# A graph layer's edge groups with a window of 97 nodes instead of 96

## The chip, the cores and the metric

The kernel runs on one core of a Trainium2 chip. The metric is the device time of one execution in microseconds (us), as the median of several runs. The core has five engines that run their own instruction streams and meet by semaphores: TensorE (PE, with its weight loads as PEld), VectorE (DVE), ScalarE (ACT), GpSimd (POOL) and SyncE (SP), and 16 DMA engines that SP, ACT and POOL feed through queues.

## The reference

One message-passing layer on a graph of 6250 nodes and 100000 edges, with features of width 128 and four attributes an edge, all in float32. Edges are sorted by their destination. Cut to what is computed:

```python
msg_in = concatenate([x[src], x[dst], edge_attr], axis=1)      # 100000 x 260
h = silu(msg_in @ mW1 + mb1)
messages = h @ mW2 + mb2
aggregated = segment_sum(messages, dst, num_segments=6250)
u = silu(concatenate([x, aggregated], axis=1) @ uW1 + ub1)
g = layer_norm(x + u @ uW2 + ub2, ln_g, ln_b)
out = layernorm(x + g)
```

## The kernel before

The first product is taken apart: `x @ mW1` is computed per node, once for the part of the source (table A) and once for the part of the destination (table B, with the bias). Both tables are written to DRAM, `tab_a` and `tab_b` (L394, L395), in seven parts of up to eight blocks of 128 nodes. After that an edge needs row A of its source, row B of its destination, and the product of its four attributes with four rows of `mW1`.

The edges are cut into 98 groups of 1024, each eight tiles of 128 edges. Because the edges are sorted, the destinations of a group lie in a window of `W` consecutive nodes that begins at the first edge's destination (`bases[g]`, a register on SP and DVE). `W` is 96. The window serves twice:

- On the way in, rows B are not gathered per edge. The window's `W` rows are loaded into `mv[g % 5][:W]` (L590), below them stand the four rows of `mW1` for the attributes. The matching matrix `stbuf[g % 5]` has `W` rows of 0 and 1 that say which edge goes to which node (`node_matrix`, L595, on DVE), and the four attribute rows of the group's edges under them (L591). One product per tile on PE (L622) gives the destination's part and the attributes' part together, over 100 rows.
- On the way out, `edge_matrix` (L608, DVE) makes the same matrix with edges on the partitions, and PE sums the messages' hidden rows `h` by node (L651), 96 columns a tile. The result is added into `acc` at the window's place (L664), the counts into `deg` (L669).

If a group's destinations go beyond the window, or a node batch would close too early, `bad_i` is set (L239 to L265), and a general path after the last group does the whole work again; with these inputs it is not entered.

What feeds this: `destinations` (L319) loads, for four groups at once, one byte an edge from `near_d`, 4096 bytes in a row, and repeats that row on all `W` partitions of the tile `near` (L324, two buffers). It is issued by SP ahead of the first of its groups' loads. `load(g)` (L584) issues the rows of B and the attributes four groups ahead. All of these go over SP's DMA queue, in SP's order, beside the node batches' loads (L499) and stores (L563) and the attributes' turning (L310, L317). A load into a buffer waits until its last reader is done.

Rows of A are gathered by POOL, one indirect DMA a tile (L281), so eight a group and 782 in all, 128 rows of 512 bytes each. `fetch(g + 2)` is issued in turn `g` of the loop over groups, and two dependencies are put on it by hand: its first gather waits for the first product of group `g + 2`, its fifth for the first summing product of group `g`. The gathers of POOL use eight semaphores in turn.

In turn `g` of the loop (L679 to L723) the order on the engines is written out by hand: the loads of group `g + 4`; the sum of gathered rows and product, `s = ga + pre` (L639, DVE), and its SiLU (L640, ACT); the products of group `g + 2` (L622, PE), whose PSUM buffer is free once `s` is computed; `node_matrix(g + 3)` and `edge_matrix(g + 1)` (DVE); the addition of group `g - 2`; the summing products of group `g` (L651, PE); then `fetch(g + 2)`. Batches of finished nodes (`node_batch`, L470) run in steps between. The first five groups are handled apart: they gather rows of `x` itself, and PE turns and multiplies them (L365, L373, L625), so that they need not wait for table A. From group 5 (`RAW`) on table A is read.

The change touches the constant `W` (L76) and, through it, the sizes of `p_next`, `w_row`, `zeros`, `acc`, `deg`, `deg_q`, `near`, `mv`, `stbuf`, `oh` and `pt`.

Of the kernel before, what the change touches and what calls it, by code (L numbers as in the profile page):

```python
# [24 lines left out]
def kernel(  # L25
# [47 lines left out]
    GE = G * P  # L73
    NG = -(-E // GE)
    assert NG <= P
    W = 96  # L76
    NW = NP + W
    K1 = W + ED
    RB = 14
# [95 lines left out]
    make_identity(nc, ident)  # L175
    w_row_i = consts.tile([P, W], I32, name="w_row_i")
    nc.gpsimd.iota(w_row_i, pattern=[[1, W]], base=0, channel_multiplier=0)

    w_row = fixed.tile([P, W], F32, name="w_row")
    nc.vector.tensor_copy(w_row, w_row_i)  # L180
# [3 lines left out]
    nc.vector.tensor_copy(p_col, p_col_i)  # L184
    p_next = consts.tile([W, 1], F32, name="p_next")
    nc.vector.tensor_scalar(p_next, p_col[:W], 1.0, None, op0=OP.add)
# [733 lines left out]
```

## Time and profile before

| | |
|---|---|
| median of three runs | 1205.35 us (1204.87 to 1210.69) |
| profiled execution | 1207.88 us |
| its span, first to last instruction | 1206.1 us |
| mean granted TensorE clock | 0.654 |
| busy: PE / DVE / ACT / POOL | 762.4 / 488.4 / 245.3 / 742.2 us |
| gathers L281, mean | 948 ns |
| loads of B (L590): number, size each | 98, 48 KB |
| loads of destinations (L324): number, size each | 24 of 384 KB and one of 192 KB |
| `node_matrix` L595, mean | 1269 ns |
| `edge_matrix` L608, mean | 949 ns |
| product L622 / summing product L651, mean of one pass | 394 / 350 ns |

A float32 product counts as two passes in the profile, so L622 and L651 have 1564 each for 782 tiles. Line numbers (L281) are those of the kernel's source. "Idle before" is the time that an engine stood still ahead of an instruction, with what ended it; "issue" means that nothing visible did, "remote" that the releasing event could not be traced to an instruction. DMA packets are recorded with queue, size, start and duration, but without the number of the DMA engine: q0 is POOL's queue, q1 SP's, q10 ACT's.

### The profile page before, as it was taken

The page shows a single profiled execution, that of the slowest core. Times are in us where ns is not written, and L with a number is a line of the kernel's source. Part 1 is how long each engine was busy: PE and PEld are TensorE (multiplying, and loading weights), DVE is VectorE, ACT ScalarE, POOL GpSimd, SP SyncE. Part 2 cuts the span into 40 slices and gives each one's busy share as a digit, 9 for nine tenths or more (in the row PEclk, how much of TensorE's full clock was granted, in tenths as well). Part 3 has the DMA queues.
Part 4 walks back from the last instruction along what each step waited for, and adds up shares of the span by engine and source line. Part 5 has one row for each costly group of instructions (what it writes and reads, how often), then busy time and mean ns, then how long its engine had stood idle before and what let it go on. Part 6 is the DMA issues. An engine that isn't in the chain of part 4 may idle for free.

```text
span 1206.1 us, 11356 instructions
## 1 busy us (share of the span) xinstructions
PE 762.4 (63%) x3655; PEld 682.4 (57%) x3655; DVE 488.4 (40%) x1023; ACT 245.3 (20%) x306; POOL 742.2 (62%) x790
## 2 busy tenths in 40 slices
PE   4656588665665766575566675666676657566564
PEld 4555577565555655465466465555566547455553
DVE  4450356353253344335335244334334326235253
ACT  1202024013022222212112122102202202112233
POOL 6446356666666666666666666666666666666660
PEclk8877777865756666666756656666655665765665
DMA  8553123212222322222222223222212312222210
GB/s 204 163 150 88 29 61 91 67 51 78 74 64 62 80 66 64 78 66 61 74 72 60 72 54 82 75 62 64 80 50 78 82 51 72 75 53 63 57 49 28
DMA packets 70221, 88.95 MB, mean 74 GB/s; under 512 B 20720, under 2 KB 51839, under 8 KB 70155
## 3 DMA queue, kind: packets, MB, share of 16 engines
q0 software_dynamic: 25024, 51.30, 16.4%
q1 hardware_dynamic: 40552, 34.96, 10.1%
q10 hardware_dynamic: 4578, 1.89, 0.7%
q8 instruction: 31, 0.51, 0.2%
q14 instruction: 36, 0.29, 0.1%
HBM read 76.71 MB, written 11.38 MB: 73 GB/s over the span
## 4 chain that ended last, share of the span: by engine, by line
PE 33%; issue 33%; POOL 15%; DVE 7%; another core or an unknown queue 7%; DMA 2%; ACT 1%; SPq 0%; ACTq 0%; DVEq 0%; POOLq 0%
POOL ga L281 15%; PE pre L622 14%; PE pt L651 12%; PE y L529 2%; DVE oh L608 1%; DMA ga<-tab_a,src_i 1%; DVE st L595 1%; PE wide L388 1%; PE y L520 1%; DVE st L487 1%; PE y L513 1%; DVE s L639 1%; PE y L514 1%; DVE deg L669 1%
## 5 line engine op out<-in xcount | busy, mean ns | idle before, releaser
L281 POOL DMA_INDIRECT ga<-tab_a,src_i x742 | 703.1, 948 | 406.2 <-issue 201.5
L622 PE MATMUL pre<-mv,st 100*128 100x128 f32 x1564 | 342.5, 394 | 243.0 <-issue 202.6
L622 PEld LDWEIGHTS pre<-mv,st 100*128 100x128 f32 x1564 | 312.6, 298 | 264.8 <-issue 227.4
L651 PE MATMUL pt<-oh,h 128*128 128x96 f32 x1564 | 294.6, 350 | 128.4 <-issue 119.3
L651 PEld LDWEIGHTS pt<-oh,h 128*128 128x128 f32 x1564 | 280.0, 266 | 146.1 <-issue 140.7
L639 DVE TENSOR_TENSOR s<-ga,pre 128x1024 f32<-128x1024 f32 x92 | 112.2, 1219 | 500.1 <-DMA ga<-tab_a,src_i 425.0
L640 ACT ACTIVATE h<-s 128x1024 f32<-128x1024 f32 x92 | 97.0, 1056 | 688.8 <-issue 424.4
L595 DVE TENSOR_SCALAR_CACHE_REDUCE st<-near,p_next 96x1024 f32<-96x1024 uint8 x98 | 124.2, 1269 | 3.0 <-DMA ea_d<-pad 1.5
L608 DVE TENSOR_TENSOR oh<-w_row,rel 128x768 f32<-128x768 f32 x98 | 93.0, 949 | 0.6 <-PE pt L651 0.6
L281 POOL DMA_INDIRECT ga<-in_x_dram,src_i x32 | 30.3, 946 | 24.4 <-PE wide L365 12.4
L531 DVE TENSOR_TENSOR y<-y,xs 128x512 f32<-128x512 f32 (+2 forms) x13 | 8.4, 647 | 86.6 <-issue 71.0
L640 ACT ACT_TABLE_LOAD x25 | 32.1, 1283 | 22.5 <-remote 17.6
L388 PE MATMUL wide<-w,xT 128*128 128x256 f32 x98 | 29.0, 462 | 11.4 <-ACT xT L344 7.3
L493 ACT ACT_TABLE_LOAD x26 | 33.4, 1283 | 4.4 <-DVE st L487 3.9
L388 PEld LDWEIGHTS wide<-w,xT 128*128 128x128 f32 x98 | 23.0, 241 | 16.2 <-ACT xT L344 7.5
L529 PEld LDWEIGHTS y<-u,uT 128*128 128x128 f32 x94 | 22.6, 324 | 11.9 <-issue 11.8
L518 ACT ACTIVATE uT<-y,ub_col 128x512 f32<-128x512 f32 (+2 forms) x13 | 8.4, 646 | 89.3 <-remote 62.2
L664 DVE TENSOR_TENSOR acc<-acc,pt 128x96 f32 x98 | 23.7, 242 | 5.7 <-remote 3.8
L529 PE MATMUL y<-u,uT 128*128 128x128 f32 x94 | 25.7, 429 | 0.0
L669 DVE TENSOR_TENSOR deg<-deg,pt 1x96 f32 x98 | 24.4, 249 | 1.0
L488 DVE BATCH_NORM_AGGREGATE mv<-st 128x2 f32<-128x6 f32 x98 | 17.8, 182 | 11.6 <-DVE st L487 5.5
L625 PE MATMUL pre<-w,ga 128*128 128x128 f32 x80 | 20.6, 344 | 3.0 <-issue 2.9
(122 smaller groups left out, 381.3 us busy)
## 6 DMA issues: line engine op xcount, KB each, us to landing
ga<-tab_a,src_i POOLq DMA_INDIRECT x742
near<-near_d SPq DMA_DIRECT2D x24, 384.0 KB
mv<-tab_b SPq DMA_DIRECT2D x98, 48.0 KB
tab_a<-t SPq DMA_DIRECT2D x6, 512.0 KB
tab_b<-x_sb SPq DMA_DIRECT2D x6, 512.0 KB
xs<-in_x_dram SPq DMA_DIRECT2D x11, 256.0 KB
out_dram<-z SPq DMA_DIRECT2D x11, 256.0 KB
st<-ea_d SPq DMA_DIRECT2D x98, 16.0 KB
```

Source lines behind the costliest of these rows:

```text
L281: ins = nc.gpsimd.indirect_dma_start(out=rows[g][:, i, :], out_offset=None, in_=x if g < RAW else tab_a[:, :], in_offset=bass.IndirectOffs ...
L388: ins = nc.tensor.matmul(pm[:, j], xT[:, cols], w1, start=True, stop=True)
L493: nc.scalar.activation(r[:, :n], mv[:, :n, 1], AF.Sqrt, bias=eps)
L529: nc.tensor.matmul(y[:, i, :], by_p[:, :, i], u2, start=False, stop=i == n - 1)
L595: nc.vector.tensor_scalar(stbuf[g % NST][:W], near.pop(g), p_next, 0.0, op0=OP.is_equal, op1=OP.add, accum_out=deg_q[g // DQ % 2][:, g % D ...
L608: nc.vector.tensor_tensor(oh, w_row[:, None, :].to_broadcast([P, G, W]), rel[:, g, :, None].to_broadcast([P, G, W]), op=OP.is_equal,)
L622: ins = nc.tensor.matmul(pre[:, i, :], st[:, i, :], mv[g % NM], start=True, stop=g >= RAW)
L639: nc.vector.tensor_add(s[:, :n], ga[:, :n], ps[:, :n])
L640: nc.scalar.activation(h[:, :n], s[:, :n], AF.Silu)
L651: ins = nc.tensor.matmul(pt[:, :W], h[:, i, :], oh[:, i, :], start=i == 0, stop=i == tiles_of(g) - 1)
L664: nc.vector.tensor_add(at, at, pt[:, :W])
L669: nc.vector.tensor_add(at, at, pt[row, W:])
```

## The change

One constant grows by one: a group's window holds 97 nodes instead of 96. Every tile, DMA and instruction that has `W` rows or columns gets 97; their number, their order on each engine and the waits between them stay as they are. Loads of B go from 96 rows of 512 bytes to 97, loads of destinations from 96 rows of 4096 bytes to 97. The product L622 runs over 101 rows, the summing product L651 has 97 columns, `edge_matrix` 776 elements a partition.

```diff
     NG = -(-E // GE)
     assert NG <= P
-    W = 96
+    W = 97
     NW = NP + W
     K1 = W + ED
     RB = 14
```

## The prediction

> **What bounds the kernel now.** I read the page first (busy shares, DMA queues, chain), then the waits, then POOL's timeline in the long middle stage, then the packet records behind the DMA view. Busy shares and DMA of the page:
>
> ```profile
> span 1206.1 us, 11356 instructions
> PE 762.4 (63%) x3655; PEld 682.4 (57%) x3655; DVE 488.4 (40%) x1023; ACT 245.3 (20%) x306; POOL 742.2 (62%) x790
> ...
> q0 software_dynamic: 25024, 51.30, 16.4%
> q1 hardware_dynamic: 40552, 34.96, 10.1%
> ```
>
> No engine is full, and the 16 DMA engines are a quarter full (26.5% for the two queues). The reason is in POOL's timeline (start, duration, line, idle before and its releaser):
>
> ```profile
> 618.12 0.95 POOL L281 DMA_INDIRECT ga<-tab_a,src_i  x1 [0.30 <-issue]
> 619.37 0.95 POOL L281 DMA_INDIRECT ga<-tab_a,src_i  x1 [0.30 <-issue]
> 623.79 0.95 POOL L281 DMA_INDIRECT ga<-tab_a,src_i  x1 [3.48 <-remote]
> ```
>
> A gather is issued every 1.25 us (0.95 + 0.30), and every 12 to 16 gathers POOL stops for 2.5 to 3.3 us more. From 205 to 1177 us there are 670 gathers: 670 x 1.25 = 838 us, and the stops fill the other 134 of the 972. So 11.6 us a group (972 / 84) is POOL's own pace. Everything else has play, which I measure in group 40 (timelines of DVE, PE, POOL):
>
> ```profile
> 519.85 1.22 DVE L639 TENSOR_TENSOR s<-ga,pre 128x1024 f32<-128x1024 f32 x1 [7.13 <-DMA ga<-tab_a,src_i]
> ...
> 521.12 3.79 PE L622 MATMUL pre<-mv,st 100*128 100x128 f32 x16 [0.50 <-issue]
> 524.86 3.18 PE L651 MATMUL pt<-oh,h 128*128 128x96 f32 x16
> ...
> 528.61 0.94 POOL L281 DMA_INDIRECT ga<-tab_a,src_i  x1 [0.30 <-issue]
> ```
>
> The sum at 519.85 starts as its gathers land; 1.3 us later PE begins the product that group 42's first gather waits for. That gather is issued at 528.61, 7.5 us after its release; its fifth would follow at 533.6, 8.7 us after the 524.86 that releases it. A third rope: gathers use eight semaphores in turn, so each waits for the landing of the one eight before, 10.0 us earlier; by the packet records a gather lands 2.2 us (median) after its issue, which leaves 7.8. Gathers may thus land about 7 us late before POOL feels it.
>
> The start is different. From the waits and the chain:
>
> ```profile
> POOL ga L281 <- DMA tab_a<-t: 10.9, 1, 10.9
> PE pre L622 <- DMA mv<-tab_b: 6.7, 1, 6.7
> ...
> 82.00 3.75 DMA near<-near_d
> ...
> 88.97 36.21 another core or an unknown queue
> ```
>
> Group 5's gathers and PE's first product stand on the last table stores and on the first load of B; up to about 205 us POOL is not the bound.
>
> **What the Trainium skill says.** "DMA: Bandwidth & Descriptors", section "Why a DMA increments its semaphore by 16 and not by 1": a transfer is split over the largest k up to 16 that divides the slowest dimension of both sides; 96 rows give 16, 127 rows give 1, and on SP's path it is the lowest-numbered k engines. 97 is prime, so k = 1, always the same engine. The trace agrees for 96: a near load has 96 packets of 4096 B at 159 ns when nothing is beside them (15.3 us in sum), yet they all end 2.1 to 4.3 us after the issue in the main stage. No DMA of before with so many rows has k = 1. The section "Queues, rings and completion order" says that an engine serves one queue in ring order and goes round the queues by packets. The first half decides the start; on the second the trace is ambiguous: a gather issued at 27.18, beside two table stores, began 2.4 us later than usual, as long as some 88 of the stores' 27 ns packets. That is more than one packet's turn.
>
> **The change part by part.**
>
> Widths. The edge matrix grows from 768 to 776 elements: 949 ns x 8/768 = 10 ns x 98 = 1 us on DVE. The 1564 passes of L651 grow by a column, 350/96 = 3.6 ns each, 5.7 us on PE. The near comparison has a partition more, same length. DVE is 40% busy and PE 63%, behind POOL's pace: 0 on the path, at most 7 us if it were all bare.
>
> Semaphore updates. 98 loads of B and 25 of near send one instead of 16: 1845 packets of 4 B fewer at 9 ns, 1 us per engine, in engines that are idle three quarters of the time: 0.
>
> Load on the one engine, per four groups: near 97 x 159 ns = 15.4 us; B 4 x 97 x 27 ns = 10.5; edge attributes 4 x 0.16 = 0.6; the gathers' share 32 x 0.23 = 7.4. Sum 33.9 of 46.3 us (73%). It keeps up; what matters is how late it is.
>
> B loads. Transfer 2.6 us instead of about 0.2: the load lands after 3.9 instead of 1.5 us. Products of the main stage start 24 to 55 us after their load's issue: 0. In the same ring behind a near load it is 16 to 19 us late, still under 24. SP can also stop while it pushes rows into a full ring (the near issue at 60.58 took 1.33 us behind two table stores, against 0.31); behind SP wait later loads, x rows and output stores, covered by the same lead.
>
> Near loads. About 18 us instead of 3 with the gathers between. Lead from issue to first use in the main stage: 25 to 47 us, but for groups 16 (12.4) and 24 (17.0). There DVE's comparison comes some 9 and 2 us late, and behind it in DVE stand the edge matrix and the sum of the next group; at group 16 that sum (218 us) moves by 1 to 2 us, inside POOL's 7. If this cover is gone, 11 us.
>
> Gathers. 8 of each gather's 128 rows go over the loaded engine, and a gather is not complete without them. If the turn is taken packet by packet, a gather waits for a few near packets, with the engine's own backlog of the size seen at the start (up to 3.7 us, with two queues full of x loads): under 7, so 0. If near's rows pass as one block, up to 15.4 us: POOL then stops 15.4 - 7.8 = 7.6 us for each of about 20 near loads of the main stage, 152 us. Below nothing: near no longer takes all engines at once, but gathers that land sooner have nobody waiting. I take +2, for moments in which PE is late as well.
>
> The start. Near load 0 is issued at 60.58, its packets run from 64.5 to 67.4. On one engine they end at 64.5 + 15.4 + six gathers x 0.25 = 81.4. Behind it in the ring are the table stores of the last 9 row blocks (72 rows x 2 tables on that engine, 144 x 27 ns = 3.9): 85.3 instead of 77.5. So tab_a is complete 8 us later, and group 5's gathers start at 86.5 instead of 78.62; the first load of B waits for tab_b, +8, and takes 2.4 us longer: PE's first product +10. Near load 4 then stands behind three more loads of B and ends near 116 instead of 85.75; its comparison and edge matrix are wanted by DVE's next work only at 125 (the 36.21 us piece of the chain), which itself moves by about 9. Bounds: 0, if that piece (PE slow from 98 to 118 us, for a cause that the profile doesn't name) ends at a fixed time; 10 if all passes on. I take 9, as PE's order is fixed and nothing in it depends on a clock.
>
> Sum: 9 + 2 = 11. The profiled execution is 1207.88 us (span 1206.1 and 1.8 around it), 0.2% over the median 1205.35: 1218.9 for such an execution, 1216.4 at the median; I say 1217.
>
> **The rivals.**
>
> *Near as a block.* The single engine serves gathers only behind what is queued before them: 1205 + 9 + 150 = about 1365. For it: the late gathers at the start. Against: those had thousands of rows beside them on all engines, and rows of 512 B, so they don't tell whether the wait is counted in rows or in bytes (at 4096 B the same bytes are 11 rows, 1.8 us).
>
> *Something between.* Blocks of at most 64 rows: 64 x 159 ns = 10.2 us, less 7.8 is 2.4 us x 20 = 48; with 9 of the start 1262. Uneven turns (several rows per gather) let gathers pile up behind near and end between 1225 and 1300 as well.
>
> *Faster.* POOL's stops, some 56 of them for 134 us after 205, might come from traffic on the engines that the 16-way splits cause. If each shrank by over 0.27 us (15 us / 56, what the start costs and 0.5% beyond), the kernel would be faster; by a half, 1205 + 9 - 67 = 1147. Against: the stops come by the count of gathers, at multiples of four, and near and B loads fall anywhere between them.
>
> *No effect.* The split doesn't depend on 97, or the start absorbs its shift: 1205.
>
> **How the numbers follow.** Hidden but for the start, 1208 to 1225: 0.44, predicted 1217. Between, 1225 to 1300: 0.24. Block, 1300 to 1400: 0.21. No effect: 0.08. Faster: 0.03. The range runs from 1208, leaving out 'no effect' and 'faster' (about 0.11), up to 1370, which leaves out a tenth. 0.5% (6 us) is about what a measurement can tell from no change: faster 0.03; same 0.10 (no effect, and the low edge of hidden); slower 0.87.
>
> **What the profile of the changed kernel would show.** The packets of a near load in one row, 15 us and more; landing of loads of B near 4 us. Group 5's gathers near 86.5 us and PE's first product near 91. POOL's pitch still 1.25 us and its stops no longer than before; the share of its waits that end with a gather's landing (5.8 us now) still small. If that wait grows to tens of us, one near load in each, the blocks are right and I am wrong; if the start doesn't move, ring order is wrong.

## The result and the profile after

The changed kernel takes 1212.31 us (median of 13 runs, 1210.97 to 1213.6); the kernel before, run beside it, takes 1205.61 us. The ratio is 1.0053, with a 95% interval of 1.0041 to 1.0065: 0.5% slower, 6.7 us. The profiled execution took 1213.6 us, its span is 1211.8 us.

The page of the changed kernel (busy shares, DMA queues):

```profile
span 1211.8 us, 11356 instructions
PE 742.7 (61%) x3655; PEld 670.0 (55%) x3655; DVE 489.3 (40%) x1023; ACT 245.5 (20%) x306; POOL 740.4 (61%) x790
...
q0 software_dynamic: 25024, 51.30, 16.3%
q1 hardware_dynamic: 38816, 35.10, 9.1%
```

The busy times hardly moved. SP's queue q1 has 1736 packets fewer and took less engine time (9.1% against 10.1%). The bytes of these loads grew by a hundredth, and their packets cost less engine time than before (a packet of 4096 B on q1 took 173 ns in the mean, 213 before). So there is not more work, it only stands on one engine. The page has no column for the engine: "one engine" is read from the times of the packets, below.

The chain and SP's timeline between 60 and 115 us show where the 6.7 us come from. In the chain (start and duration) stand SP's issues of the last table stores, and at 93.86 a wait of DVE for the destinations of group 4, whose last row starts at 116.7 us by the packet records:

```profile
77.70 2.18 SPq L395
...
79.98 3.46 SPq L394
...
84.02 3.00 DMA ea_d<-pad
...
93.86 23.72 issue
...
119.75 14.14 another core or an unknown queue
```

SP's timeline of the same execution (start, duration):

```profile
62.16 1.06 SPq L324 DMA_DIRECT2D near<-near_d  x1
72.86 0.37 SPq L394 DMA_DIRECT2D tab_a<-t  x1
73.69 6.19 SPq L395 DMA_DIRECT2D tab_b<-x_sb  x1
79.98 3.46 SPq L394 DMA_DIRECT2D tab_a<-t  x1
83.55 0.38 SPq L395 DMA_DIRECT2D tab_b<-x_sb  x1
...
86.85 0.28 SPq L590 DMA_DIRECT2D mv<-tab_b  x1
```

The same place in the kernel before:

```profile
73.67 1.19 SPq L394 DMA_DIRECT2D tab_a<-t  x1
74.96 1.19 SPq L395 DMA_DIRECT2D tab_b<-x_sb  x1
...
78.06 0.36 SPq L590 DMA_DIRECT2D mv<-tab_b  x1
```

The first load of destinations is issued at 62.16. When SP wants to issue the last table stores, that load's rows are still being worked off (67.0 to 83.1 us by the packet records; before, 64.6 to 67.4): the issue at 73.69 takes 6.19 us, the next 3.46. This is best read as SP waiting for room in a full ring, a queue's list of pending packets on one DMA engine (e1, below, has neither). The first load of B leaves SP at 86.85 instead of 78.06.

In the main stage nothing was lost. Group 40 in the timelines of DVE, PE and POOL, as it was shown of the kernel before:

```profile
529.01 1.22 DVE L639 TENSOR_TENSOR s<-ga,pre 128x1024 f32<-128x1024 f32 x1 [8.61 <-DMA ga<-tab_a,src_i]
...
531.93 3.59 PE L622 MATMUL pre<-mv,st 101*128 101x128 f32 x16 [1.63 <-issue]
...
535.48 2.45 PE L651 MATMUL pt<-oh,h 128*128 128x97 f32 x16
...
532.29 0.94 POOL L281 DMA_INDIRECT ga<-tab_a,src_i  x1 [2.54 <-remote]
...
537.28 0.94 POOL L281 DMA_INDIRECT ga<-tab_a,src_i  x1 [0.30 <-issue]
```

POOL still issues every 1.25 us and still has its stops. Group 42's first gather follows its release by 5.4 us (537.28 less 531.93) where it was 7.5 before. Over groups 18 to 95 the median of this play is 7.7 us (9.7 before) and the smallest 4.4: it has shrunk, and is not used up. Worked out from the instructions of both traces, in us (group 16 is the first whose gathers run at POOL's own pace):

```
                                          before    after
first gather of group 5                     78.6     87.4   (+8.8)
PE's first product                          81.0     92.0  (+11.0)
first gather of group 16                   228.5    236.4   (+7.9)
from there to the first gather of group 96 928.9    926.5   (-2.4)
from there to the end                       48.7     48.9   (+0.2)
last gather issued to sum started, median   2.67     5.12   (groups 16 to 96)
```

The last row is how late the gathers have become: 2.45 us at the median, as long as some 15 rows of destinations. The packet records show what happens on the engine. Around the load of destinations that SP issued at 445.98, in us:

```
q1  512 B x 97    446.89 to 449.17   rows of B, 23.5 ns from one to the next
q1 4096 B x 98    449.18 to 466.05   destinations (97) and a row of attributes, 163 ns each
q0 4096 B         between them, about 13 gathers' shares of 0.2 us on the same engine
```

97 rows, one after the other, for 16.9 us: this is k = 1. The gathers' shares pass in between, one at a time.

### The profile page after: what moved, and what is told of

Its sections match the earlier page's. It is cut to its first block, busy times and chain, and to the rows that moved or that the text cites. A ratio compares the mean times of both kernels' runs of the same rounds, so it can differ in the third digit from the quotient of the medians.

```text
span 1211.8 us, 11356 instructions
## 1 busy us (share of the span) xinstructions
PE 742.7 (61%) x3655; PEld 670.0 (55%) x3655; DVE 489.3 (40%) x1023; ACT 245.5 (20%) x306; POOL 740.4 (61%) x790
## 4 chain that ended last, share of the span: by engine, by line
issue 33%; POOL 26%; PE 26%; DVE 5%; another core or an unknown queue 4%; DMA 4%; ACT 1%; SPq 1%; DVEq 0%; POOLq 0%; ACTq 0%
POOL ga L281 26%; PE pre L622 10%; PE pt L651 9%; DMA ga<-tab_a,src_i 3%; PE wide L388 2%; PE y L529 1%; DVE st L595 1%; PE wide L343 1%; DVE oh L608 1%; PE y L513 1%; PE y L520 1%; DVE s L639 1%; PE y L514 1%; PE y L515 0%
## 5 line engine op out<-in xcount | busy, mean ns | idle before, releaser
L622 PE MATMUL pre<-mv,st 101*128 101x128 f32 x1564 | 337.1, 392 | 295.3 <-issue 218.3
L622 PEld LDWEIGHTS pre<-mv,st 101*128 101x128 f32 x1564 | 309.4, 297 | 313.9 <-issue 248.1
L651 PE MATMUL pt<-oh,h 128*128 128x97 f32 x1564 | 285.2, 345 | 97.7 <-issue 81.6
L651 PEld LDWEIGHTS pt<-oh,h 128*128 128x128 f32 x1564 | 273.3, 264 | 110.6 <-issue 100.2
L595 DVE TENSOR_SCALAR_CACHE_REDUCE st<-near,p_next 97x1024 f32<-97x1024 uint8 x98 | 124.6, 1273 | 40.4 <-issue 30.6
L608 DVE TENSOR_TENSOR oh<-w_row,rel 128x776 f32<-128x776 f32 x98 | 94.1, 961 | 0.0
L664 DVE TENSOR_TENSOR acc<-acc,pt 128x97 f32 x98 | 24.2, 247 | 5.7 <-PE pre L622 3.8
L669 DVE TENSOR_TENSOR deg<-deg,pt 1x97 f32 x98 | 24.5, 250 | 1.0
L391 DVE TENSOR_TENSOR x_sb<-wide,b 128x512 f32<-128x512 f32 (+1 forms) x13 | 8.2, 653 | 31.4 <-ACT t L390 27.8
```

The lines of the kernel that those rows point to most:

```text
L595: nc.vector.tensor_scalar(stbuf[g % NST][:W], near.pop(g), p_next, 0.0, op0=OP.is_equal, op1=OP.add, accum_out=deg_q[g // DQ % 2][:, g % D ...
L608: nc.vector.tensor_tensor(oh, w_row[:, None, :].to_broadcast([P, G, W]), rel[:, g, :, None].to_broadcast([P, G, W]), op=OP.is_equal,)
L622: ins = nc.tensor.matmul(pre[:, i, :], st[:, i, :], mv[g % NM], start=True, stop=g >= RAW)
L651: ins = nc.tensor.matmul(pt[:, :W], h[:, i, :], oh[:, i, :], start=i == 0, stop=i == tiles_of(g) - 1)
L664: nc.vector.tensor_add(at, at, pt[:, :W])
L669: nc.vector.tensor_add(at, at, pt[row, W:])
```

## Experiments

Three theories were on the table. *Start*: all the loss comes before the main stage, from loads of destinations that are wanted soon after their issue. *Spread*: each of the 25 loads costs a little, or the loads of B do. *Widths*: 97 columns and 101 rows cost time on PE and DVE. The runs were made in three sets of four, each on its own chip with the kernel before beside it; the kernel before took 1190.62 us, 1016.21 us and 1205.86 us there, so ratios are compared, and times only within a set.

**e1, only the first load split.** The first load of destinations goes as 96 rows and one row.

```diff
-        nc.sync.dma_start(
-            t[:, :n].rearrange("w g e -> w (g e)"), flat.to_broadcast([W, n * GE])
-        )
+        to = t[:, :n].rearrange("w g e -> w (g e)")
+        for lo, hi in ((0, 96), (96, 97)) if g == 0 else ((0, W),):
+            nc.sync.dma_start(to[lo:hi], flat.to_broadcast([hi - lo, n * GE]))
```

> W stays 97; only the first load of destinations goes as 96 rows and one row, all later ones and all loads of B stay on one engine. Theory (the loss is all made before 205 us, by the first load of destinations standing ahead of the last table stores on one engine): group 5's gathers begin near 79 us again instead of 87.4, PE's first product near 84 instead of 92, and 1204 to 1207 us, no longer slower than before by more than 2 us. Rival (the loss is spread over the main stage, a bit with every load of destinations): stays at 1210 to 1213.

Measured: 1189.27 us, ratio 0.9987 (0.9975 to 0.9999). SP's timeline of e1:

```profile
71.44 0.38 SPq L394 DMA_DIRECT2D tab_a<-t  x1
72.27 0.39 SPq L395 DMA_DIRECT2D tab_b<-x_sb  x1
72.76 1.09 SPq L394 DMA_DIRECT2D tab_a<-t  x1
73.94 1.19 SPq L395 DMA_DIRECT2D tab_b<-x_sb  x1
...
77.11 0.28 SPq L590 DMA_DIRECT2D mv<-tab_b  x1
```

The stores go out at once, group 5's gathers begin at 77.6 us and PE's first product at 82.2. One load of 25 undone, and the loss is gone, though 24 loads of destinations and 98 of B still stand on one engine. Gathers are as late as in the changed kernel (5.08 us), and the main stage is no longer for it: from group 16 to 96 it is 920.9 us, and 921.1 in e4, where all loads are split.

**e2, destinations alone.** W = 96; the tile `near` has 97 rows and every load fills them (lines between are left out).

```diff
-        t = work.tile([W, NQ, GE], U8, name="near")
+        rows = 97 if True else W
+        t = work.tile([97, NQ, GE], U8, name="near")
...
-            t[:, :n].rearrange("w g e -> w (g e)"), flat.to_broadcast([W, n * GE])
+            t[:rows, :n].rearrange("w g e -> w (g e)"), flat.to_broadcast([rows, n * GE])
...
-            near[g + k] = t[:, k, :]
+            near[g + k] = t[:W, k, :]
```

> The kernel before, W = 96, but each load of destinations brings 97 rows (the last is not read): that part of the change alone, rows of B still over all engines. Theory: the start shifts by 8 us at the gathers of group 5, 1210 to 1213 us in all. Rival (the rows of B, or the wider tiles, make the loss): 1205 to 1207.

Measured: 1197.78 us, ratio 1.0070 (1.0055 to 1.0086). Destinations alone make a loss as large as the whole change's (7.2 us here, 6.7 on the first chip). Group 5's gathers begin 4.9 us later than in e1 (82.5).

**e3, B split.** W = 97, destinations on one engine, each load of B in two.

```diff
-        nc.sync.dma_start(mv[g % NM][:W], tab_b[bass.ds(bases[g], W), :])
+        nc.sync.dma_start(mv[g % NM][:96], tab_b[bass.ds(bases[g], 96), :])
+        nc.sync.dma_start(mv[g % NM][96:W], tab_b[bass.ds(bases[g] + 96, 1), :])
```

> W = 97, every load of rows of B goes as 96 rows and one row, loads of destinations stay on one engine. Theory: rows of B cost at most the 2.4 us of the first product, so 1209 to 1213 us, near the changed kernel's 1212.3. Rival (rows of B make the loss): 1205 to 1207.

Measured: 1201.47 us, ratio 1.0104 (1.0086 to 1.0122). Sending B over all engines gains nothing; the loss is, if anything, larger than the changed kernel's, which ran on the other chips only (ratios 1.0053 and 1.0058).

**e4, both split.** The edits of e1, for every load, and of e3 together: all loads over many engines, so that the widths remain, and 123 more loads of one row.

> W = 97 with all loads of destinations and of B as 96 rows and one row: the wider tiles alone, and 123 more small loads. Theory: widths are hidden behind POOL's pace, 1204 to 1208 us, the same as before. Rival (97 columns and 101 rows cost time on PE and DVE): 1210 or more.

Measured: 1193.76 us, ratio 1.0033 (1.0015 to 1.0051). The expectation of "the same" is missed by a little. e3 against e2 and e4 against e1 differ by about 4 us each, both times in the kernel whose loads of B are split; by the profiles 2.7 and 3.2 us of it are there at group 16. So it is likely the further issue for each load of B, with its register work on SP, that costs; e12 below takes the widths apart from it. The pair e3 and e4 gives the price of destinations on one engine once more: 7.7 us.

**e5, the load doubled.** Each load of destinations but the first is issued a second time into a tile that nobody reads. **e6** does so with 96 rows in place of both 97s, over all engines.

```diff
+        if g:
+            more = work.tile([97, NQ, GE], U8, name="more")    # e6: 96
+            nc.sync.dma_start(
+                more[:, :n].rearrange("w g e -> w (g e)"), flat.to_broadcast([97, n * GE])
+            )
```

> The changed kernel, with every load of destinations but the first issued a second time, into a tile that nobody reads, also 97 rows: 15.4 us more on the one engine for each four groups, 49.3 instead of 33.9 against POOL's 46.3. Theory (one engine carries the loads, free of charge as long as its sum stays under POOL's pace): now the engine is the bound, the main stage takes (49.3 + 1 for other transfers) / 46.3 of its time, 6 to 15% more in all. Rival (the loads are hidden for another reason than the engine's spare time, such as their early issue): 0 to 1% over the changed kernel.

> The same with the second load of 96 rows, over all engines: as many bytes and as many issues as in e5, 1 us an engine. Theory: 0 to 0.5% over the changed kernel, so 0.5 to 1% over the kernel before. If e5's loss comes from issues on SP or from bytes, this one loses as much.

Measured: e5 1249.75 us, ratio 1.2298 (1.2278 to 1.2318); e6 1064.4 us, ratio 1.0465 (1.0445 to 1.0485). From group 16's first gather to group 96's it is 938.5 us in e5, 46.9 us for four groups, and 802.4 us in e6, 40.1 us for four groups. The waits of e5 (total, times, longest, in us):

```profile
DVE s L644 <- DMA ga<-tab_a,src_i: 563.0, 83, 18.4
PE pre L627 <- DMA st<-ea_d: 260.0, 21, 15.4
...
POOL ga L281 <- PE pre L627: 204.9, 30, 23.9
...
DVE st L600 <- DMA near<-near_d: 74.3, 17, 23.7
```

PE now waits for loads behind the doubled ones in the ring, and POOL for PE. The same bytes over all engines leave the main stage at POOL's pace (640 gathers x 1.25 us = 800). So one engine's time is what counts. The sum for e5 with the row times seen on the chip (destinations 2 x 15.4, B 4 x 2.3, attributes 0.6, gathers 7.4) is 48 us, and 46.9 were measured. The expected excess of 6 to 15% was sized for a pace of 46.3 us; this chip's pace is 40, and over e7, which is the changed kernel but for one issue, e5 takes 18% more. e6 missed its figure of 0.5 to 1% over the kernel before: on this chip the changed loads cost more without any doubling (e7).

**e7, first load in another ring.** The changed kernel with the first load of destinations issued by ACT.

```diff
-        nc.sync.dma_start(
+        (nc.sync if g else nc.scalar).dma_start(
```

> The changed kernel, with the first load of destinations issued by ACT, so in another ring of the same one engine, and the table stores no longer behind it. Theory (ring order makes the start's loss): the last table stores share the engine with it turn by turn and end near 81 instead of 85 us, gathers of group 5 near 83, and a third to two thirds of the loss is gone: 0.1 to 0.4% over the kernel before. Rival (the engine serves all rings in order of arrival): as the changed kernel, 0.5%.

Measured: 1055.68 us, ratio 1.0391 (1.0371 to 1.0410). A miss. Group 5's gathers begin at 71.1 us, against 70.5 in e5 and 74.5 in e6, where SP issues that load: no gain. The packet records of e7 show why. From 50 to 60 us, 49 rows of destinations (q10, 4096 B) and 49 table stores (q1, 512 B) start, always one of the former after one of the latter; two pairs of them, start in us:

```
50.554 q1 512 B    50.578 q10 4096 B    50.733 q1 512 B    50.756 q10 4096 B
```

So the engine serves the two rings in turn, a packet at a time, 179 ns for a row and a store, and not in order of arrival. The turns that the expectation assumed were right; its working was wrong. Each store waits for one row, and the engine has more stores to do (144 of the last row blocks alone) than the 97 rows, so the stores end last, after the whole sum, whichever ring the rows are in. SP was held up as well: its store at 49.12 took 10.94 us to issue.

What e6 and e7 show besides is the size of the loss on this chip: about 4% with the changed loads, in the start alone. Their main stages take 802.4 and 801.2 us, that of e8 (below) 800.7, while e7 is 12.6 us behind e8 at group 5 and 34.6 us at group 16. In between the chain of e7 runs through two more loads of destinations, for groups 8 and 16, and through a long issue of SP:

```profile
113.58 21.75 DMA near<-near_d
...
148.19 12.87 SPq L591
...
176.10 21.93 DMA near<-near_d
```

How much of this the loads of B on the same engine add was not separated on this chip.

**e8, later loads alone.** W = 96, first load over all engines, later loads of 97 rows (lines between are left out).

```diff
-        t = work.tile([W, NQ, GE], U8, name="near")
+        rows = 97 if g else W
+        t = work.tile([97, NQ, GE], U8, name="near")
...
-            t[:, :n].rearrange("w g e -> w (g e)"), flat.to_broadcast([W, n * GE])
+            t[:rows, :n].rearrange("w g e -> w (g e)"), flat.to_broadcast([rows, n * GE])
...
-            near[g + k] = t[:, k, :]
+            near[g + k] = t[:W, k, :]
```

> The kernel before, W = 96, its first load of destinations over all engines, the later ones with 97 rows on one engine. Theory: no shift of the start; in the main stage POOL's issue of a gather is not slowed (945 instead of 948 ns) by loads that use all engines at once, so 0 to 0.3% faster than before. Rival (later loads cost): slower than before.

Measured: 1020.23 us, ratio 1.0037 (1.0024 to 1.0049). Slower, not faster: a miss. The chain of e8 points to a cause, and it isn't in the main stage:

```profile
54.78 3.16 DMA tab_b<-x_sb
61.90 20.71 DMA near<-near_d
```

That is the load for group 4, the second one, issued at 61.90: here the chain runs through it for 20.71 us. So later loads of the start can count too. How many of the 4 us are its own is open, since the kernel before has no profile on this chip.

**e9 to e12, on a third chip.** e9 is the changed kernel and e10 the kernel before, unedited. e11 is e1 with the condition `g < 16`: the loads for groups 0 to 15 are split. e12 has the window at 112.

```diff
-    W = 97
+    W = 112
```

> The changed kernel as it is, to have it on the same chip as the next three. e5 to e8 ran on a chip where the kernel before takes 1016 us and POOL's stops are missing. Theory (the loss lies before the main stage, and how much of it shows depends on how busy PE and POOL were there without it): where the kernel before takes about 1016 us, 3.5 to 5% slower, with the main stage as long as before within 3 us; where it takes 1190 us or more, 0.3 to 0.8% slower. Rival (the loss is the same everywhere, 7 us): 0.7% slower also where the kernel before takes 1016 us.

> The kernel before, for its profile on the same chip: on a chip that takes about 1016 us for it, group 5's gathers near 58 us and group 16's near 170; on one that takes about 1200, near 78 and 225.

> W = 97, the loads of destinations for groups 0 to 15 as 96 rows and one row, all later ones and all loads of B on one engine. Theory: only early loads of destinations cost, because their lead is short; within 0.6% of the kernel before on any chip. Rival (loads of B on one engine or later loads of destinations cost a good part where POOL has no stops): half of e9's loss or more stays.

> W = 112: all loads over all engines again, but sixteen columns and rows more than before instead of one. Theory (widths are hidden behind POOL's pace in the main stage): PE's summing pass 350 to about 400 ns, DVE's edge matrix 949 to 1107 ns, and 0.1 to 0.8% slower, from the start alone. Rival (PE or DVE is close to the bound): 2% or more, and one column would then have cost 0.1% or more.

Measured: e9 1213.14 us, ratio 1.0058 (1.0041 to 1.0075); e10 1208.64 us, one run; e11 1194.97 us, ratio 0.9936 (0.9915 to 0.9957); e12 1204.84 us, ratio 0.9993 (0.9966 to 1.0019). From the profiles, in us:

```
                        group 5   PE's first  group 16   16 to 96   end
e10 kernel before          79.5      81.9       229.3      930.1    1206.8
e9  changed                86.3      90.9       235.6      928.9    1211.2
e11 early loads split      75.2      79.6       211.1      928.9    1186.8
e12 window of 112          74.8      77.3       222.1      929.9    1199.4
```

Here the loss is as in the first runs: 6.3 us of it are there at group 16 (235.6 less 229.3), and none is added after. At 0.58%, e9 lies where it was expected for such a chip; for a chip of about 1016 us the expectation was not put to a test, since the changed kernel itself never ran there.

e12 settles the widths. With sixteen columns and rows more, the main stage is as long as before, and the loss of 0.1 to 0.8% that was expected from the start is not seen. The loads of destinations are over all engines again: by the packet records most of them end 3 to 5 us after their issue, against 17 to 22 in the changed kernel. Two groups of e12's instructions (line, engine, shapes, busy time, mean ns):

```profile
L651 PE MATMUL pt<-oh,h 128*128 128x112 f32 x1564 | 284.4, 339 | 137.6 <-issue 129.2 <-ACT h L734 4.7 <-DVE deg L669 1.4
...
L608 DVE TENSOR_TENSOR oh<-w_row,rel 128x896 f32<-128x896 f32 x98 | 106.3, 1085 | 1.4 <-remote 1.4
```

The edge matrix takes 136 ns more (949 before); the summing pass took 339 ns against 353 in e10, where 400 were expected. Part of that is the clock: e12's mean granted clock was 0.699, e10's 0.657. At the same clock the passes are nearly equal: where all 16 of a group ran at the full granted clock, they took 1.94 us in e12 (median of 30 groups) and 1.92 in e10 (of 21), under 1% more for a sixth more columns.

e11 is the best version: 0.64% faster than the kernel before and 1.5% under the changed one beside it. That the loss goes was expected; that it becomes a gain was not. Its 20 runs spread from 1188.9 to 1206.4 us, wider than those of the kernel before (six are at 1202 or above), and its profile, which is of the fastest of them, is shorter than e10's between groups 5 and 16 (135.9 us against 149.8). The windows from 75 to 225 us of e11 and of e10 (columns: window, its length, busy time with instructions of PE, PE's weight loads, DVE, ACT and POOL, granted clock, DMA share, GB/s):

```profile
75.00:225.00 150.00, 105.36 (x670) 97.42 (x670) 66.35 (x135) 30.11 (x38) 93.50 (x100) 0.77 0.27 75
```

```profile
75.00:225.00 150.00, 104.79 (x625) 97.11 (x624) 65.61 (x136) 28.27 (x36) 82.10 (x87) 0.73 0.29 77
```

PE is busy the same 105 us in both, but e11 gets 670 instructions done in them instead of 625, at a granted clock of 0.77 instead of 0.73. Why the clock is higher there was not found, so the gain of e11 stays partly open.

## Why the prediction was right

**What bounds the kernel: right.** POOL's pace set the main stage in every version but e5, and its length hardly moved with the change (926.5 against 928.9 us, 928.9 against 930.1).

**Ring order at the start: right.** Group 5's gathers were put at 86.5 us and came at 87.4; PE's first product was put at 91 and came at 92.0. The load for group 4 was put to end near 116; DVE's comparison, which waits for it, began at 117.6. e1 and e2 show the cause by undoing it and by doing it alone. e7 adds that sharing a ring is not what matters: issued into another ring, the load delays the stores just as long, since the engine has the same sum to do. The waits of the changed kernel show the comparison for group 4:

```profile
DVE st L595 <- issue: 30.6, 2, 23.7
```

Its 23.7 us were covered, as the prediction said, by the stretch in which PE is slow: in the chain an unknown piece still follows, 14.14 us where it was 36.21.

**Leads: right.** The comparison for group 16 was to come 9 us late; it moved from 205.6 to 223.3, 9.8 us more than the start's shift, and POOL didn't feel it: the first gathers of groups 14 to 24 all begin 7.9 to 8.1 us later than before. e8 shows what the cover is worth where it is thin.

**Gathers: right that they are hidden.** The block did not come: a gather is 2.45 us later at the median, under the 7 us of play. That an engine goes round its queues by packets, as the Trainium skill says in "Queues, rings and completion order" ("DMA: Bandwidth & Descriptors"), fits what was seen: single shares of gathers stand between the rows, and in e7 rows and stores alternate 49 to 49. The wait is still longer than one row's turn, some 15 rows; why was not found, as for the delay beside table stores that made the prediction doubt. e5 shows the limit that was left: the engine's sum against POOL's pace, 73% of it in the changed kernel by the prediction's estimate.

**Sizes.** The sum was 9 + 2 = 11 us against 6.7 measured (5.7 between the spans). The 2 us for gathers that meet a late PE were not there: the main stage was 2.4 us shorter in the first pair of profiles and 1.2 in the second, which is too little to call a gain. Of the 9 us of the start, 7.9 arrived at group 16. The story that came true had been given 0.44, and its slower rivals, a block or something between, 0.45 together; the range up to 1370 was theirs.

**What the prediction left out** is how much the start's loss depends on what else fills the start. It named the slow PE as a bound on it and took the leads of later loads as cover. On the chip of e5 to e8, where the start is faster (group 5 at 58.5 us in e8), loads on one engine cost some 4%, and the chain of e7 goes through later loads of destinations as well.

## What to carry to other kernels

Here one row more put a whole load on one DMA engine: 97 rows stood on one, 96 and 112 on all. With such a load, add up that engine's time per turn of the loop and compare it with the pace of the bound; it may be free. What costs is latency: look for loads used soon after their issue, and for whatever else that engine has to do then, stores included, in whichever ring. Splitting off the odd row of only those few loads was enough to win back the loss, of one load in e1 and of four in e11.

## What the runs showed of the hardware

- The same kernel took 1205.6, 1190.6, 1016.2 and 1205.9 us beside the four sets of runs. On the chip of 1016 us POOL's stops are missing. Waits of POOL between 205 and 990 us in e8:

```profile
POOL ga L281 <- issue: 176.4, 579, 0.3
POOL ga L281 <- DMA ga<-tab_a,src_i: 7.6, 25, 0.3
```

  No wait there is longer than 0.3 us, and groups 16 to 96 take 800.7 us, 640 x 1.25; in e9 and e10 the stops are worth some 129 us of the same stretch. What makes them was not found; the kernel before ran unedited on all these chips.
- SP stands still while, as it is best read, one engine's ring is full: issues that usually take 0.3 us took 6.19 and, for attributes behind the second load of destinations, 12.87 us in the changed kernel. On SP a load over one engine thus also delays what is issued after it for other engines; issued by ACT (e7), it held up an issue of SP for 10.94 us as well.
- One DMA engine with work in the rings of SP and ACT took one packet of each in turn: 49 rows of 4096 B and 49 of 512 B in 10 us of e7.
- PE's summing pass hardly grows with its columns from 96 to 112: 1.92 and 1.94 us for 16 passes at the full granted clock.
